# A scheduler's duration table in a cross-attention and MoE-LoRA kernel, with transposes modelled as holding the SP queue

## The chip, the core and the metric

The kernel runs on one core of a Trainium2 chip. The metric is the device time of one execution in microseconds (us). One execution was also recorded by the hardware profiler; the profile's lines come from it. Engine names in the profile are PE (TensorE matmul), PEld (its weight load), DVE (VectorE), ACT (ScalarE), POOL (GpSimd) and SP (SyncE, which here only issues DMAs).

## What is computed

There are two batches of 1024 rows; rows are 2048 wide. `fake_quant` rounds to 0..255 and scales back.

```
x = x + fake_quant(layernorm(x)) @ fake_quant(ctx)        # GEMM 1, 2048 x 2048 per batch
y = layernorm(x)
w = top-2 softmax weights of y @ W_router.T               # 8 experts, rank 16
x = x + y @ W_base.T + b_base + 2 * sum_e w_e (y @ A_e.T) @ B_e.T    # GEMM 2 with LoRA
```

## The kernel before

**Tasks and a planner.** The kernel does not issue instructions as it goes through its loops. Each helper adds a task to a `Plan` (L88): an engine, an assumed duration, the tiles that it reads and writes, and for a DMA an assumed transfer time. `rank` gives each task a due time, counted back from the due times of its matmuls. `order` (L141) then plays the tasks through in modelled time: whenever an engine is modelled as free, it takes the ready task with the earliest due time whose tile slots are free. The tasks are emitted in the order of their modelled starts (L1133), so each engine's program order is what the model found best. The hardware keeps that order on each engine; an engine that waits for one tile holds up everything behind it. An elementwise scaling (`affine`, L339) may run on ACT or on DVE; DVE takes it only where the model has ACT busy. 3048 tasks are ordered.

The model of a DMA has three numbers: how long SP is busy issuing (0.47 us for a load, 1.25 for a transpose), how long the transfer takes on one shared DMA resource (`dma_free`: the bytes at 360e3 a us; a transpose 0.896 us per 1024 columns), and when its tile counts as landed (2.0 after). At most 8 transfers are outstanding, and none is issued when the resource is booked more than 2.5 us ahead.

**All loads, stores and transposes go through SP's one queue, in one order.** That is the order around which the change works.

**GEMM 1.** For each batch x is loaded in row tiles of 128, its mean and variance are taken on DVE (`stats`), the inverse root by Newton steps on POOL, ACT quantises it to u8 (`q8`), `qn` is the f16 copy without the zero point, and an SP transpose makes `at`, the stationary operand. The context is loaded (`bs`), quantised on DVE (`u`, L357), made f16 on ACT or DVE (`b`, L346 or L355). `gemm1` (L630) issues 128x128x512 matmuls into one of 8 PSUM banks (`g`) and DVE adds the result to x (L657).

**GEMM 2** is a Strassen-like product. For each pair p of row tiles, `y_prep` (L725) normalises four blocks of x (`yt_a`) and forms the sums s1 to s4. Each of a11, a12, a22, s1, s2, s3 and s4 is split into a high and a low f16 half (`nat_a`, `nat_s`: the copy is L346 on ACT, the subtraction L742 on DVE) and transposed by SP (L336) into `y_a` or `y_s`. `comb` is L749. x tiles are stored to DRAM (`spill`) and loaded again later (`xr`).

The weights come in rows. For each of two column halves cp, four groups grp (0 to 3) and eight steps k, `w_step` (L889) loads `wt` and `wb` (or `ws`), combines them on DVE (L918; L928 and L932; L939 and L942 by group), scales the high half (L346 on ACT or L353 on DVE) and computes the low half on DVE (L902). `g2` (L1021) runs the three matmuls per product (L1032) for the four row pairs, and after the last step adds the LoRA product (L1046) and lets DVE add the banks X and Y to x (L1057). Names like "grp 1 tile k" below mean the weight tile of that group and step.

**Router.** `hmm` (L780) multiplies y_a and y_s with the LoRA and router matrix (`ph`, L790 and L794, 16 narrow matmuls each), ACT copies and DVE adds the halves into `hf` (L806, L809). After the last of them the softmax and the top-2 weights run, and one SP transpose makes `hT`. `load_lb` prepares the LoRA output weights (`lb`), `add_bias` adds the bias to the x tiles (L978).

The first row tile is preceded by 30 warm-up matmuls (L609).

Of the kernel before, what the change touches and what calls it, by code (L numbers as in the profile page):

```python
# [21 lines left out]
P = 128  # L22
# [6 lines left out]
KT = D // P  # L29
# [14 lines left out]
MM = 0.216  # L44
# [7 lines left out]
EV1 = 5.0  # L52
SP_D = 10.0
HC = 4.0
PUT = 10.0
# [10 lines left out]
HOP = 0.7  # L66
DMA_SLACK = 3.0


# [13 lines left out]
class Task:  # L83
    __slots__ = ("eng", "dur", "durs", "fn", "preds", "succs", "prio", "cap", "bufs", "left",
                 "ready", "start", "done", "dma", "seq", "pe", "far", "need")


class Plan:  # L88
    def __init__(self):
        self.tasks = []  # L90

    def add(self, eng, dur, fn, r=(), w=(), prio=None, cap=None, dma=None, far=None):
# [7 lines left out]
        t.far = far  # L100
# [24 lines left out]
        self.tasks.append(t)  # L125
        return t
# [14 lines left out]
    def order(self):  # L141
# [51 lines left out]
        while todo:  # L193
# [8 lines left out]
            for eng in busy:  # L202
                while busy[eng] <= now:
# [66 lines left out]
def xattn_ffn_kernel(ctx, tc, x, cx, scal, wT, bias, arT, bT, out):  # L270
# [60 lines left out]
    def load(dst, dst_ap, src, nbytes, w, r=(), **kw):  # L331
        add("SP", 0.47, lambda: nc.sync.dma_start(dst_ap(), src() if callable(src) else src),
            r=r, w=w, dma=nbytes * P / 360e3, **kw)

    def transpose(dst, src, r, w, cols, **kw):
        add("SP", 1.25, lambda: nc.sync.dma_start_transpose(dst(), src()),  # L336
            r=r, w=w, dma=0.896 * cols / 1024, **kw)

    def affine(dst, src, n, r, w, scale=None, bias=None, only=None, **kw):  # L339
        ptrs = sum(v is not None and not isinstance(v, float) for v in (scale, bias))  # L340

        def fn(eng):
            get = lambda v: v() if callable(v) else v
            o, i, a, c = dst(), src(), get(scale), get(bias)
            if eng == "ACT":
                nc.scalar.activation(  # L346
                    o, i, AF.Copy if c is None else AF.Identity,
                    scale=1.0 if a is None else a, bias=0.0 if c is None else c,
                )
# [12 lines left out]
        return add(durs, 0, fn, r=r, w=w, **kw)  # L362
# [46 lines left out]
    def prep_lora(when):  # L409
# [59 lines left out]
        for q in range(2):  # L469
            s1, s2 = a32[q], a32[q + 2]  # L470
            split(s1, q)
            split(s2, q + 2)
            add("DVE", 0.6,
                lambda s1=s1, s2=s2: nc.vector.tensor_tensor(
                    s1.ap(), s2.ap(), s1.ap(), ALU.subtract), r=[s2], w=[s1])
            split(s1, q + 4)

    def prep_bmax():
        m = buf("sm", [P, 52], F32, "sm_bmax")
        for h in range(2):  # L480
            s = buf("u", [P, HD], F32, f"bms_{h}")
            load(s, s.ap, bT[:, h * HD : (h + 1) * HD], HD * 4, [s])
            add("DVE", 1.13,
                lambda s=s, h=h: nc.vector.tensor_reduce(
                    m.ap()[:, h : h + 1], s.ap(), AX.X, ALU.max, apply_absolute_value=True),
                r=[s], w=[m])
# [26 lines left out]
    def w_norm(cp, when):  # L513
        acc = buf("wacc", [P, 24], F32, f"wacc_{cp}", KT)
        for n, k in enumerate(range(KT - 1, -1, -1)):
# [6 lines left out]
            def sq(eng, s=s, d=d, k=k):  # L522
# [7 lines left out]

            add({"ACT": 1.2, "DVE": 1.3}, 0, sq, r=[s], w=[d, (acc, [k])],
                prio=when + WN_STEP * n)
# [33 lines left out]
    def ln1(S, b, i):  # L566
# [3 lines left out]
        for h in range(2):  # L570
            add("DVE", 1.2, lambda h=h: stats(xt[h], s, 0, h), r=[xt[h]], w=[s])
        add("DVE", 0.8, lambda: rstd_seed(s, 1), w=[s])
# [57 lines left out]
    def gemm1(S, b, i, c, t):  # L630
# [29 lines left out]

        add("DVE", 0.78, evac, r=[ps], w=[(xb, [c % 2]), (s, [j])], cap=t + KT * MM + EV1)
        if c % 2 == 0:
# [19 lines left out]
        sq = buf("q8", [P, HD], U8, f"sq_{b}_{i}_{c}")  # L682
        add("ACT", 1.3, lambda: square(c // 2), r=[xb], w=[(s, [j]), sq])

# [40 lines left out]
    def y_prep(S, b, p):  # L725
# [10 lines left out]
        def emit(o, t):  # L736
# [3 lines left out]
            affine(lambda: n.ap()[:, 0], t.ap, HD, [t], [n])  # L740
            add("DVE", 1.13,
                lambda: nc.vector.tensor_tensor(  # L742
# [5 lines left out]
        def comb(dst, a, c, op):  # L748
            add("DVE", 1.13, lambda: nc.vector.tensor_tensor(dst.ap(), a.ap(), c.ap(), op),  # L749
                r=[a, c], w=[dst])  # L750
# [138 lines left out]
    def w_step(S, b, cp, grp, k):  # L889
# [10 lines left out]
        def lo(src, lo, up, r):  # L900
            add("DVE", 0.14 + 0.00104 * (up - lo),
                lambda: nc.vector.scalar_tensor_tensor(  # L902
                    w.ap()[:, 1, lo:up], src(), g, w.ap()[:, 0, lo:up], ALU.mult,
                    ALU.subtract),
                r=r + [sc_r], w=[w])
# [10 lines left out]
        if grp == 0:  # L916
            add("DVE", 0.6,
                lambda: nc.vector.tensor_tensor(  # L918
# [3 lines left out]
        elif grp == 1:  # L922
# [3 lines left out]
                 C * 4, [(bot, [1])])  # L926
            add("DVE", 0.6,
                lambda: nc.vector.tensor_tensor(  # L928
                    bot.ap()[:, :C], top.ap()[:, :C], top.ap()[:, C:], ALU.subtract),
                r=[top], w=[(bot, [0])])  # L930
            add("DVE", 0.6,
                lambda: nc.vector.tensor_tensor(  # L932
# [3 lines left out]
        else:  # L936
            bot = load_wrow(HK + k, cp, f"wb_{n}", far=WFAR)
            add("DVE", 1.13,
                lambda: nc.vector.tensor_tensor(bot.ap(), bot.ap(), top.ap(), ALU.subtract),  # L939
                r=[top], w=[bot])  # L940
            add("DVE", 0.6,
                lambda: nc.vector.tensor_tensor(  # L942
# [4 lines left out]
    def load_lb(S, b, cp, js):  # L947
        s = buf("u", [P, HD], F32, f"lbs_{b}_{cp}_{js[0]}")
        load(s, s.ap, bT[:, cp * HD : (cp + 1) * HD], HD * 4, [s])
        for j in js:  # L950
# [5 lines left out]
            if j == 2:  # L956
                add("DVE", 0.6,
                    lambda: nc.vector.tensor_tensor(
                        s.ap()[:, :C], s.ap()[:, :C], s.ap()[:, C:], ALU.subtract), w=[s])
            g = sB[:, cp : cp + 1]  # L960
            add("ACT", 0.62,
                lambda lb=lb, src=src: nc.scalar.activation(
                    lb.ap()[:, 0], src(), AF.Copy, scale=g), r=[s, (scale_b, [cp])], w=[lb])
            add("DVE", 0.67,
                lambda lb=lb, src=src: nc.vector.scalar_tensor_tensor(
# [4 lines left out]
    def add_bias(S, b, cp, t):  # L970
# [4 lines left out]
        for i in [2 * p + 1 for p in range(NP)] + [2 * p for p in range(NP)]:  # L975
            xb = S["c", cp, i]
            add("DVE", 1.13,
                lambda xb=xb: nc.vector.tensor_tensor(xb.ap(), xb.ap(), bb.ap(), ALU.add),  # L978
# [12 lines left out]
    def put(S, b, cp, i, t):  # L991
        xb = S["c", cp, i]
        last = b == NB - 1 and cp == 1 and i % 2 == 0
        for c in range(2):
# [4 lines left out]
            else:  # L999
                cs, parts = slice(0, HD), [0, 1]  # L1000
            add("SP", 0.47,
                lambda cs=cs: nc.sync.dma_start(
                    out[b, i * P : (i + 1) * P, cp * HD + cs.start : cp * HD + cs.stop],
                    xb.ap()[:, cs]),
                r=[(xb, parts)], dma=4 * (cs.stop - cs.start) * P / 360e3, prio=t + PUT)

# [14 lines left out]
    def g2(S, b, cp, grp, k, p, t):  # L1021
# [30 lines left out]
        for bk, tt, c in EVAC[grp] + ((("Y", 0, 1),) if split and not grp else ()):  # L1052
# [7 lines left out]

            add("DVE", 0.72, ev, r=[ps, (scale_b, [cp])], w=[(xb, [c])], cap=t + EV2)
        if grp == 2:
# [125 lines left out]
```

## Time and profile before

| | us |
|---|---|
| three runs | 967.72, 965.92, 967.12 |
| their median | 967.12 |
| span of the profiled execution | 965.8 |
| PE busy in it | 913.9 |
| DVE, ACT, POOL busy | 734.1, 379.9, 100.0 |
| DMA, mean rate | 252 GB/s |

A line "L1032 PE ..." is a group of instructions of line 1032 of the kernel. An idle time in brackets with "<-" is the time for which the engine had nothing to do before the instruction, and what ended it. A line of a waits view reads: engine and line, what it waited for, us in total, times, longest. "SPq" is SP's queue: the instruction's duration there is the time for which it held the queue. A clock of 0.50 in a row means that a matmul takes twice as long.

### The profile page before, as it was taken

What the parts mean: (1) busy time and instruction counts of PE and PEld (TensorE: products, weight loads), DVE (VectorE), ACT (ScalarE), POOL (GpSimd) and SP (SyncE); (2) the same over time, 40 slices, a digit from 0 to 9 for tenths busy, and PEclk for the clock granted to TensorE, in tenths of its full rate; (3) what the DMA queues carried; (4) which work ended last, traced back from release to release, by engine and by line L of the source; (5) the groups of instructions that cost most, each with busy time, mean ns of one, the idle gap of its engine ahead of it and who ended that gap; (6) DMA issues with size and microseconds to landing.
All of it is one profiled execution on the core that took longest, in us unless ns stands there. A gap on an engine that the chain in (4) does not pass through costs nothing.

```text
span 965.8 us, 12426 instructions
## 1 busy us (share of the span) xinstructions
PE 913.9 (95%) x4478; PEld 431.5 (45%) x4478; DVE 734.1 (76%) x1229; ACT 379.9 (39%) x440; POOL 100.0 (10%) x353
## 2 busy tenths in 40 slices
PE   3699998997999999999999999997898999999998
PEld 1245445454444444444444444545543444444443
DVE  7579887996988876999555778987597876699231
ACT  3466785641425422243555644641230321225000
POOL 3405431000000000005220223000000000000000
PEclk9799999999999999999999999999999999999999
DMA  9999999899899986966999979899978479695011
GB/s 319 246 392 336 303 313 243 214 189 233 246 302 389 360 312 244 363 219 242 239 273 356 319 190 228 245 215 185 255 180 262 163 272 325 207 356 171 34 66 66
DMA packets 225518, 243.12 MB, mean 252 GB/s; under 512 B 160944, under 2 KB 162992, under 8 KB 225456
## 3 DMA queue, kind: packets, MB, share of 16 engines
q1 hardware_dynamic: 225456, 242.33, 83.0%
q8 instruction: 35, 0.57, 0.2%
q14 instruction: 27, 0.22, 0.1%
HBM read 172.03 MB, written 31.46 MB: 211 GB/s over the span
## 4 chain that ended last, share of the span: by engine, by line
PE 62%; DVE 19%; POOL 6%; DMA 5%; issue 5%; ACT 2%; SPq 1%; DVEq 0%; POOLq 0%; ACTq 0%
PE X L1032 28%; PE Y L1032 19%; PE g L636 11%; DVE yt_a L749 2%; DVE nat_s L742 2%; DVE w L902 2%; PE X L1046 2%; PE Y L1046 2%; DVE nat_a L742 2%; DMA wb<-in_wT_dram 2%; DVE xr L1057 1%; POOL sm L399 1%; POOL sm L395 1%; DMA wt<-in_wT_dram 1%; DVE x L657 1%
## 5 line engine op out<-in xcount | busy, mean ns | idle before, releaser
L636 PE MATMUL g<-b,at 128*128 128x512 f16 x1024 | 228.5, 386 | 9.2 <-ACT b L346 7.4
L1032 PEld LDWEIGHTS <-y_s 128*128 128x128 f16 x1536 | 149.8, 98 | 192.4 <-issue 9.9
L1032 PE MATMUL Y<-w,y_s 128*128 128x512 f16 x768 | 207.1, 380 | 5.7 <-DVE hf L809 2.8
L1032 PE MATMUL X<-w,y_s 128*128 128x512 f16 x768 | 207.7, 381 | 4.3 <-DVE w L902 2.6
L1032 PE MATMUL X<-w,y_a 128*128 128x512 f16 x768 | 190.4, 380 | 4.5 <-DVE w L902 2.6
L1032 PEld LDWEIGHTS <-y_a 128*128 128x128 f16 x1152 | 112.5, 98 | 144.9 <-issue 7.3
L636 PEld LDWEIGHTS <-at 128*128 128x128 f16 x1024 | 101.4, 99 | 133.6 <-issue 17.5
L346 ACT ACTIVATE w<-wb,gW 128x1024 f16<-128x1024 f32 x59 | 67.4, 1147 | 190.3 <-DVE wb L932 94.3
L1032 PE MATMUL Y<-w,y_a 128*128 128x512 f16 x384 | 103.3, 379 | 3.8 <-DVE xr L1057 2.7
L902 DVE SCALAR_TENSOR_TENSOR w<-wb,gW,w 128x1024 f16<-128x1024 f32 x64 | 81.6, 1278 | 11.7 <-ACT w L346 11.3
L357 DVE TENSOR_SCALAR u<-bs,rec,sc 128x1024 uint8<-128x1024 f32 x64 | 50.9, 808 | 27.5 <-DMA bs<-in_cx_dram 22.0
L346 ACT ACTIVATE b<-u,nz 128x1024 f16<-128x1024 uint8 x47 | 53.0, 1143 | 44.7 <-DVE u L357 40.2
L1057 DVE SCALAR_TENSOR_TENSOR xr<-X,uW,xr 128x512 f32<-128x512 f32 x70 | 50.5, 744 | 25.7 <-PE X L1046 23.2
L1057 DVE SCALAR_TENSOR_TENSOR xr<-Y,uW,xr 128x512 f32<-128x512 f32 x45 | 33.2, 742 | 36.0 <-PE Y L1046 36.0
L657 DVE SCALAR_TENSOR_TENSOR x<-g,s,x 128x512 f32<-128x512 f32 x64 | 47.4, 745 | 10.3 <-PE g L636 10.1
L346 ACT ACTIVATE q<-x,sm 128x1024 uint8<-128x1024 f32 x32 | 38.0, 1232 | 34.0 <-POOL sm L584 29.2
L928 DVE TENSOR_TENSOR wb<-wt 128x512 f32<-128x512 f32 x32 | 21.9, 687 | 34.4 <-DMA wt<-in_wT_dram 28.7
L939 DVE TENSOR_TENSOR wb<-wb,wt 128x1024 f32<-128x1024 f32 x32 | 38.7, 1218 | 11.5 <-DMA wb<-in_wT_dram 11.5
L742 DVE TENSOR_TENSOR nat_s<-yt_a,nat_s 128x1024 f16<-128x1024 f32 x32 | 38.3, 1217 | 5.5 <-ACT nat_s L346 5.5
L367 DVE BATCH_NORM_STATS2 sm<-x 128x6 f32<-128x512 f32 x64 | 40.4, 680 | 2.5 <-DMA x<-in_x_dram 2.4
L346 ACT ACTIVATE nat_s<-yt_a 128x1024 f16<-128x1024 f32 x27 | 27.8, 1049 | 33.3 <-DMA y_s<-nat_s 14.9
L790 PE MATMUL ph<-ar,y_a 128*128 128x272 f16 x192 | 37.0, 284 | 3.9 <-DVE xr L1057 2.1
(157 smaller groups left out, 901.8 us busy)
## 6 DMA issues: line engine op xcount, KB each, us to landing
wt<-in_wT_dram SPq DMA_DIRECT2D x88, 512.0 KB, 6.4
bs<-in_cx_dram SPq DMA_DIRECT2D x64, 512.0 KB, 9.9
wn<-in_wT_dram SPq DMA_DIRECT2D x32, 512.0 KB, 7.6
wb<-in_wT_dram SPq DMA_DIRECT2D x32, 512.0 KB, 8.1
x<-in_x_dram SPq DMA_DIRECT2D x30, 512.0 KB, 8.3
spill<-x SPq DMA_DIRECT2D x28, 512.0 KB, 4.0
xr<-spill SPq DMA_DIRECT2D x28, 512.0 KB, 6.8
out_dram<-xr SPq DMA_DIRECT2D x24, 512.0 KB, 4.2
```

The source lines that it names most:

```text
L346: nc.scalar.activation(o, i, AF.Copy if c is None else AF.Identity, scale=1.0 if a is None else a, bias=0.0 if c is None else c,)
L357: nc.vector.tensor_scalar(o, i, a, c, ALU.mult, ALU.add)
L367: nc.vector.bn_stats(st[:, 2 * h + c], b.ap()[:, c * C : (c + 1) * C])
L636: nc.tensor.matmul(ps.ap(), aT.ap()[:, k, :], S["b", c, k // 4].ap()[:, k % 4, :], start=k == 0, stop=k == KT - 1,)
L657: nc.vector.scalar_tensor_tensor(xs, ps.ap(), s12, xs, ALU.mult, ALU.add, accum_out=s.ap()[:, o : o + 1])
L742: lambda: nc.vector.tensor_tensor(n.ap()[:, 1], t.ap(), n.ap()[:, 0], ALU.subtract), r=[t], w=[n])
L790: nc.tensor.matmul(ph.ap()[:, : 2 * AR], y[half].ap()[:, 0, k, :], ar[:, kr, :], start=kk == 0, stop=False,)
L902: lambda: nc.vector.scalar_tensor_tensor(w.ap()[:, 1, lo:up], src(), g, w.ap()[:, 0, lo:up], ALU.mult, ALU.subtract),
L939: lambda: nc.vector.tensor_tensor(bot.ap(), bot.ap(), top.ap(), ALU.subtract),
L1032: nc.tensor.matmul(ps.ap(), y.ap()[:, a, k, :], w.ap()[:, q, j * C : (j + 1) * C], start=k == 0 and fresh and i == 0, stop=k == HK - 1 and ...
L1046: nc.tensor.matmul(ps.ap(), hT.ap()[:, 2 * p + tt, a], lb.ap()[:, q], start=False, stop=i == 2, skip_group_check=True,)
L1057: nc.vector.scalar_tensor_tensor(xs, ps.ap(), uW[:, cp : cp + 1], xs, ALU.mult, ALU.add)
```

## The change

Only numbers and rules of the planner change. No task is added or removed, none does other work; the program's order and the choice between ACT and DVE follow from the new model. The line numbers of the kernel after are larger by 3 to 7.

- A transpose is modelled as holding SP until the modelled transfers ahead of it are through and its own time (0.35 + 0.6 us per 1024 columns) has passed; its tile lands 2.4 us later. Before, it held SP 1.25 us whatever was ahead.
- Another DMA holds SP 0.4 us for 0.47, starts 0.2 us after issue (1.1 after its start before), moves 405e3 bytes a us for 360e3, and lands 1.8 us later for 2.0.
- Most DVE durations and three ACT durations in the table grow by 0.03 to 0.18 us. PE's and POOL's are left.

```
+RATE = 405e3
+LAND = 1.8
+TURN_LAND = 2.4
...
                     end = now + t.dur
-                    busy[eng] = end
-                    wake(end)
                     if t.dma is not None:
-                        dma_free = max(now + 1.1, dma_free) + t.dma
-                        t.done = dma_free + 2.0
+                        if t.turn:
+                            dma_free = end = max(now + 0.3, dma_free) + t.dma
+                            t.done = dma_free + TURN_LAND
+                        else:
+                            dma_free = max(end + 0.2, dma_free) + t.dma
+                            t.done = dma_free + LAND
                         lanes = [x for x in lanes if x > now] + [t.done]
                     else:
                         t.done = end + 0.2
+                    busy[eng] = end
+                    wake(end)
                     wake(t.done)
...
     def load(dst, dst_ap, src, nbytes, w, r=(), **kw):
-        add("SP", 0.47, lambda: nc.sync.dma_start(dst_ap(), src() if callable(src) else src),
-            r=r, w=w, dma=nbytes * P / 360e3, **kw)
+        add("SP", 0.4, lambda: nc.sync.dma_start(dst_ap(), src() if callable(src) else src),
+            r=r, w=w, dma=nbytes * P / RATE, **kw)
 
     def transpose(dst, src, r, w, cols, **kw):
         add("SP", 1.25, lambda: nc.sync.dma_start_transpose(dst(), src()),
-            r=r, w=w, dma=0.896 * cols / 1024, **kw)
+            r=r, w=w, dma=0.35 + 0.6 * cols / 1024, turn=True, **kw)
...
-        durs = {"ACT": n * 0.00083 + 0.19 + 0.09 * ptrs, "DVE": n * 0.00053 + 0.08 + 0.06 * ptrs}
+        durs = {"ACT": n * 0.00083 + 0.19 + 0.09 * ptrs, "DVE": n * 0.00053 + 0.145 + 0.06 * ptrs}
```

The other durations that change, each in its own line: a DVE subtraction or addition of 1024 columns (L742, L749, L939, L978) and the reduction in the preparation 1.13 to 1.22; one of 512 columns (L918, L928, L932, L942, L958) 0.6 to 0.69; `stats` 1.2 to 1.38; GEMM 1's eviction L657 0.78 to 0.84; GEMM 2's eviction L1057 0.72 to 0.75; L902 0.14 to 0.215 plus 0.00104 a column; the squares 1.3 to 1.33 (ACT, L675) and 1.2 and 1.3 to 1.25 and 1.31 (ACT and DVE); `lb` 0.62 to 0.72 (ACT) and 0.67 to 0.75 (DVE).

More of the change, by code (lines that the diff above doesn't have):

```diff
@@ L84 @@
     __slots__ = ("eng", "dur", "durs", "fn", "preds", "succs", "prio", "cap", "bufs", "left",
-                 "ready", "start", "done", "dma", "seq", "pe", "far", "need")
+                 "ready", "start", "done", "dma", "seq", "pe", "far", "need", "turn")
 class Plan:
@@ L90, in __init__, with add @@
         self.tasks = []
-    def add(self, eng, dur, fn, r=(), w=(), prio=None, cap=None, dma=None, far=None):
+    def add(self, eng, dur, fn, r=(), w=(), prio=None, cap=None, dma=None, far=None, turn=False):
         t = Task()
@@ L99, in add @@
         t.pe = prio if eng == "PE" else None
-        t.far = far
+        t.far, t.turn = far, turn
         def spans(accs):
@@ L472, in prep_lora @@
             split(s2, q + 2)
-            add("DVE", 0.6,
+            add("DVE", 0.69,
                 lambda s1=s1, s2=s2: nc.vector.tensor_tensor(
@@ L482, in prep_bmax @@
             load(s, s.ap, bT[:, h * HD : (h + 1) * HD], HD * 4, [s])
-            add("DVE", 1.13,
+            add("DVE", 1.22,
                 lambda s=s, h=h: nc.vector.tensor_reduce(
@@ L529, in sq @@
                     )
-            add({"ACT": 1.2, "DVE": 1.3}, 0, sq, r=[s], w=[d, (acc, [k])],
+            add({"ACT": 1.25, "DVE": 1.31}, 0, sq, r=[s], w=[d, (acc, [k])],
                 prio=when + WN_STEP * n)
@@ L570, in ln1 @@
         for h in range(2):
-            add("DVE", 1.2, lambda h=h: stats(xt[h], s, 0, h), r=[xt[h]], w=[s])
+            add("DVE", 1.38, lambda h=h: stats(xt[h], s, 0, h), r=[xt[h]], w=[s])
         add("DVE", 0.8, lambda: rstd_seed(s, 1), w=[s])
@@ L659, in evac @@
             )
-        add("DVE", 0.78, evac, r=[ps], w=[(xb, [c % 2]), (s, [j])], cap=t + KT * MM + EV1)
+        add("DVE", 0.84, evac, r=[ps], w=[(xb, [c % 2]), (s, [j])], cap=t + KT * MM + EV1)
         if c % 2 == 0:
@@ L682, in gemm1 @@
         sq = buf("q8", [P, HD], U8, f"sq_{b}_{i}_{c}")
-        add("ACT", 1.3, lambda: square(c // 2), r=[xb], w=[(s, [j]), sq])
+        add("ACT", 1.33, lambda: square(c // 2), r=[xb], w=[(s, [j]), sq])
     def ln2(S, b, p):
@@ L740, in emit @@
             affine(lambda: n.ap()[:, 0], t.ap, HD, [t], [n])
-            add("DVE", 1.13,
+            add("DVE", 1.22,
                 lambda: nc.vector.tensor_tensor(
@@ L748, in comb @@
         def comb(dst, a, c, op):
-            add("DVE", 1.13, lambda: nc.vector.tensor_tensor(dst.ap(), a.ap(), c.ap(), op),
+            add("DVE", 1.22, lambda: nc.vector.tensor_tensor(dst.ap(), a.ap(), c.ap(), op),
                 r=[a, c], w=[dst])
@@ L900, in lo @@
         def lo(src, lo, up, r):
-            add("DVE", 0.14 + 0.00104 * (up - lo),
+            add("DVE", 0.215 + 0.00104 * (up - lo),
                 lambda: nc.vector.scalar_tensor_tensor(
@@ L916, in w_step @@
         if grp == 0:
-            add("DVE", 0.6,
+            add("DVE", 0.69,
                 lambda: nc.vector.tensor_tensor(
@@ L926, in w_step @@
                  C * 4, [(bot, [1])])
-            add("DVE", 0.6,
+            add("DVE", 0.69,
                 lambda: nc.vector.tensor_tensor(
@@ L930, in w_step @@
                 r=[top], w=[(bot, [0])])
-            add("DVE", 0.6,
+            add("DVE", 0.69,
                 lambda: nc.vector.tensor_tensor(
@@ L937, in w_step @@
             bot = load_wrow(HK + k, cp, f"wb_{n}", far=WFAR)
-            add("DVE", 1.13,
+            add("DVE", 1.22,
                 lambda: nc.vector.tensor_tensor(bot.ap(), bot.ap(), top.ap(), ALU.subtract),
                 r=[top], w=[bot])
-            add("DVE", 0.6,
+            add("DVE", 0.69,
                 lambda: nc.vector.tensor_tensor(
@@ L956, in load_lb @@
             if j == 2:
-                add("DVE", 0.6,
+                add("DVE", 0.69,
                     lambda: nc.vector.tensor_tensor(
@@ L960, in load_lb @@
             g = sB[:, cp : cp + 1]
-            add("ACT", 0.62,
+            add("ACT", 0.72,
                 lambda lb=lb, src=src: nc.scalar.activation(
                     lb.ap()[:, 0], src(), AF.Copy, scale=g), r=[s, (scale_b, [cp])], w=[lb])
-            add("DVE", 0.67,
+            add("DVE", 0.75,
                 lambda lb=lb, src=src: nc.vector.scalar_tensor_tensor(
@@ L976, in add_bias @@
             xb = S["c", cp, i]
-            add("DVE", 1.13,
+            add("DVE", 1.22,
                 lambda xb=xb: nc.vector.tensor_tensor(xb.ap(), xb.ap(), bb.ap(), ALU.add),
@@ L1000, in put @@
                 cs, parts = slice(0, HD), [0, 1]
-            add("SP", 0.47,
+            add("SP", 0.4,
                 lambda cs=cs: nc.sync.dma_start(
@@ L1004, in put @@
                     xb.ap()[:, cs]),
-                r=[(xb, parts)], dma=4 * (cs.stop - cs.start) * P / 360e3, prio=t + PUT)
+                r=[(xb, parts)], dma=4 * (cs.stop - cs.start) * P / RATE, prio=t + PUT)
     GROUPS = (
@@ L1059, in ev @@
                 )
-            add("DVE", 0.72, ev, r=[ps, (scale_b, [cp])], w=[(xb, [c])], cap=t + EV2)
+            add("DVE", 0.75, ev, r=[ps, (scale_b, [cp])], w=[(xb, [c])], cap=t + EV2)
         if grp == 2:
```

## The prediction

> **What bounds the kernel now.** I read the page's busy times first, then busy time by stage, then waits, chain and timelines of the stages where TensorE (PE) is not full.
>
> ```profile
> span 965.8 us, 12426 instructions
> ...
> PE 913.9 (95%) x4478; PEld 431.5 (45%) x4478; DVE 734.1 (76%) x1229; ACT 379.9 (39%) x440; POOL 100.0 (10%) x353
> ```
>
> PE is without work for 965.8 - 913.9 = 52 us. A change of order can only move these, or time in which PE ran at half clock. Busy time by stage (columns: stretch, its length, PE, PEld, DVE, ACT, POOL, clock, DMA share, GB/s) says where they are:
>
> ```profile
> 0.00:47.00 47.00, 23.25 (x68) 8.60 (x69) 31.33 (x71) 19.31 (x17) 18.03 (x62) 0.85 0.95 280
> ...
> 160.00:205.00 45.00, 39.95 (x211) 19.26 (x209) 43.13 (x75) 23.67 (x26) 0.40 (x1) 1.00 0.94 224
> 205.00:245.00 40.00, 34.52 (x225) 19.66 (x224) 32.10 (x44) 10.40 (x14) 0.00 (x0) 0.96 0.96 227
> ...
> 620.00:694.00 74.00, 64.03 (x400) 35.92 (x399) 55.09 (x84) 23.59 (x28) 0.00 (x0) 0.98 1.00 238
> 694.00:745.00 51.00, 48.26 (x223) 21.59 (x222) 42.20 (x81) 12.15 (x13) 0.00 (x0) 1.00 0.77 221
> ```
>
> PE misses 23.8 us in startup, 5.1 + 5.5 in batch 0's change of GEMM, 10.0 + 2.7 in batch 1's; from 325 to 620 it is busy throughout. Next, what the SP queue does in these stages: the transposes' line (min/median/max of one, ns), and SP's timeline.
>
> ```profile
> L336 SPq DMA_TRANSPOSE y_s<-nat_s x32: 1359/2500/8552, 137.7 to 722.7; - x32
> ```
>
> ```profile
> 217.44 14.10 SPq L336 DMA_TRANSPOSE y_s<-nat_s  x5
> 231.60 0.83 SPq L332 DMA_DIRECT2D wt<-in_wT_dram  x1
> ```
>
> Five transposes hold the queue 14.1 us (2.8 each; the planner believed 1.25), and the weight load behind them leaves at 231.60. DVE, whose next instruction needs it, stands. The same follows in batch 1, here in the chain (start, length, what):
>
> ```profile
> 680.51 5.71 DMA wt<-in_wT_dram
> 686.25 0.70 DVE wb L928
> ...
> 726.15 6.46 DMA wb<-in_wT_dram
> ...
> 733.85 1.40 DVE xr L1057 x2
> ```
>
> PE's timeline has the price, in brackets on the right:
>
> ```profile
> 690.47 0.81 PE L1032 MATMUL Y<-w,y_s 128*128 128x512 f16 x3 [2.79 <-DVE hf L809]
> ```
>
> ```profile
> 734.65 0.82 PE L1032 MATMUL Y<-w,y_a 128*128 128x512 f16 x3 [1.89 <-DVE xr L1057]
> ```
>
> PE did not wait for that weight tile: it waited for short DVE work (the router's add L809, the evictions L1057) that the planner had put behind the DVE instruction that waited for the load:
>
> ```profile
> 732.70 1.22 DVE L939 TENSOR_TENSOR wb<-wb,wt 128x1024 f32<-128x1024 f32 x1 [6.29 <-DMA wb<-in_wT_dram]
> 733.85 0.74 DVE L1057 SCALAR_TENSOR_TENSOR xr<-Y,uW,xr 128x512 f32<-128x512 f32 x1
> ```
>
> **The change part by part.** No instruction's work changes and none is added or taken out: 3048 tasks before and after. So every duration edit has no cost of its own, and acts through the order and the choice of ACT or DVE alone. Set side by side task by task, PE keeps 1103 of 1269 places (no move over 14 places), SP 389 of 503 (none over 4), POOL all. DVE and ACT change most: 42 tasks go from DVE to ACT, 28 the other way. I take each stage where PE waits, follow the new order through the old durations, and count the change in PE's time.
>
> *Startup, 0 to 47.* Three more cx loads go ahead of the first transpose (landing near 24.5 for 20.4), and half a dequantised b tile goes behind a q pass on ACT, so the first real matmuls start near 38 instead of 31.05. But the last b tile no longer stands behind both normalised rows, so PE then runs on, without the 3.43 us it waited until 41.27. By 46.9 I count 36 to 37 matmuls both ways: **0**, bounds -2 and +3.
>
> *85 to 112.* Two of the at transposes go behind stores and wn loads; at number 4 is issued near 91.1 for 85.9. Its first use had 4.9 us of slack, its successors 2.4 to 3.2: 0 if all slack holds, +3 if one misses by its slack again. I take **0**, nearest to the slack rows; the next stage swallows a little lateness anyway.
>
> *160 to 245.* The first weight tile of GEMM 2 is late already: PE's waits for L902 are 5.2 us in three.
>
> ```profile
> PE X L1032 <- DVE w L902: 5.2, 3, 2.6
> ```
>
> In the new order the subtraction L918 and a copy stand with L902 on DVE, 1.4 us more, for a DVE that is 43.13 of 45 us busy. Behind it the transposes still precede the same wt load, and L902 of the third grp 1 tile goes behind L928 and L932 of later tiles (0.69 + 0.69 a pair): ready near 243.4 for 241.8. That wait is behind all the earlier ones, so it alone counts: **+1.6**, bounds -2 (the y_s waits of 205 to 245 shrink) and +5 (it adds to the 1.4 and the slack lost before).
>
> *245 to 325.* One gap of 0.43 us goes (a wb load passes a transpose). Three hi copies move to ACT, but DVE takes L939 of tiles 6 and 7 (1.22 each) ahead of L902 of tile 5, which comes to 305.0 where PE wanted it at 302.9: +2.1 - 0.43, **+1.6**, bounds -1 and +3. From 325 to 620 the nearest slack I found is 8.6 us: 0.
>
> *628 to 694.* The evictions L1057 of group 0 go ahead of two nat_s subtractions (1.22 each): the gap of 2.06 us at 658 falls to some 0.6, **-1.5**. The router's adds L809 and the last three evictions go ahead of the L928 that waits for the wt load: PE's gaps of 1.85, 0.98, 2.79 and 0.52 (6.1) go. What is late next is the y_s2 tile of rows 2 and 3, whose transpose is itself in the queue; I charge one hold, the row's median 2.5: **-3.6**. Bounds for both together -7.6 (nothing late next) and -1 (each gap has a new owner).
>
> *725 to 740.* The wt and wb loads of tile 2 pass the last y_s3 transpose, and the evictions stand ahead of L939: gaps of 1.89, 0.33 and 0.52 go, **-2.7**, bounds -2.7 and 0. The tail, 3.8 us of eviction and store after the last matmul, stays.
>
> Sum: 0 + 0 + 1.6 + 1.6 - 1.5 - 3.6 - 2.7 = -4.6 on the profiled execution: 965.8 to 961.2. The runs' median is 967.12, 1.3 above that span, so **962.5**.
>
> The clock is left at 0 in this sum. It fell to half right after the gap at 658:
>
> ```profile
> 661.30:664.70 3.40, 3.40 (x18) 2.13 (x17) 3.03 (x4) 0.00 (x0) 0.00 (x0) 0.50 0.04 7
> ```
>
> 3.4 us at 0.50 cost 1.7. If the gap caused it, its going saves 1.7; a new gap elsewhere may cost as much: bounds -1.7 and +1.7, and 0 stands midway. [...]
>
> [...]
>
> **The rivals.**
>
> *Batch 1's gain comes whole.* Nothing is late after the removed stalls (-1.5 - 6.1 - 2.7 = -10.3) and batch 0 costs 1 to 3: 965.8 - 8.3 + 1.3 = 958.8; with batch 0 neutral and the clock's 1.7 saved, 955. For it: the holds are the same in both batches, and PE's gaps there are all DVE order. Against: between 620 and 694 the DMA share is 1.00, so the next transpose is never far.
>
> *No change.* The wt load still stands behind the transposes (SP moves nothing over 4 places), DVE still idles 7 us for it, and each removed PE wait is taken over by the next late tile: batch 1 gives -3, batch 0 takes +3: 967.
>
> *Slower: DVE's weight work becomes the bound of batch 0.* Where the new order puts L939 and L942 of later tiles (1.22 + 0.69) ahead of L902 of the tile that PE wants, each such step without slack costs PE 1.9 us. 160 to 325 has some 24 steps and DVE is 146 of 165 us busy. Four such steps are +7.6; with half of batch 1's gain (-3.9), 967.12 + 3.7 = 970.8. It decides from three late steps on, if batch 1 gives no more than half. For it: two such steps are in my sum already. Against: between 245 and 325 PE lost only 1.1 us so far.
>
> *The model doesn't hold.* It makes every transpose wait for the modelled transfers ahead, but one of 1024 columns at 14.53 was through in 1.3 us with loads outstanding; then the order is shuffled without aim: between the last two cases.
>
> **How the numbers follow.** This kernel's measurement tells about 0.2% (1.9 us) from no change, so same is 965.2 to 969.0. The forecast, batch 0 a few us late and batch 1 most of its gaps rid, 960 to 965: 0.43. The whole gain, below 960: 0.17. No change: 0.13. Slower, 969 to 974: 0.27. The range 955.5 to 970.5 takes the whole gain down to its end, and the slower case up to four late steps; the forecast's own range is 958.5 to 965.
>
> **What would show it.** Right: no PE waits for L809 at 665 to 693, and none for xr L1057 behind L939 at 730; DVE idles for wt and wb loads as before, 28.7 and 11.5 us, without PE behind it; PE's waits for L902 grow from 5.2 us to some 8. Wrong: PE waits for y_s grow in batch 1 by more than 2.5 us; the start of real matmuls after 40 us; at transposes that PE waits for near 96; or more than three waits for L902 between 245 and 325.

## The result and the profile after

The kernel after takes 972.54 us (median of 4 runs, 970.43 to 972.85), before 967.42 in the runs beside it: a ratio of 1.0051, interval 1.0037 to 1.0066. It is slower by half a per cent; the forecast was faster by as much. The page's first lines of after:

```profile
span 970.5 us, 12450 instructions
...
PE 913.2 (94%) x4478; PEld 430.3 (44%) x4478; DVE 728.5 (75%) x1217; ACT 395.2 (41%) x452; POOL 91.1 (9%) x353
```

PE does the same 913 us of work and stands 57 us for 52. Busy time by stage of after (stretch, length, PE, PEld, DVE, ACT, POOL, clock, DMA share, GB/s):

```profile
47.00:160.00 113.00, 108.82 (x537) 52.77 (x536) 86.30 (x207) 80.08 (x107) 28.66 (x113) 0.98 1.04 305
160.00:205.00 45.00, 38.35 (x226) 19.91 (x224) 40.04 (x70) 28.72 (x32) 0.40 (x1) 1.00 0.87 211
205.00:245.00 40.00, 34.24 (x231) 19.74 (x230) 30.73 (x38) 9.13 (x12) 0.00 (x0) 1.00 0.98 206
245.00:325.00 80.00, 73.27 (x323) 32.26 (x323) 67.54 (x108) 35.43 (x46) 0.00 (x0) 0.96 0.93 296
...
620.00:694.00 74.00, 72.10 (x486) 42.36 (x484) 62.12 (x94) 32.68 (x39) 0.00 (x0) 1.00 0.97 219
```

Batch 1's change of GEMM is cured (72.10 of 74 for 64.03). But 47 to 160, where PE never stood before, has lost 4.2, and 245 to 325 now 6.7 for 1.1. Which waits are new, PE's waits of after say (total, times, longest):

```profile
PE g L643 <- DMA at<-qn: 6.3, 2, 4.2
PE g L643 <- ACT b L353: 5.3, 2, 3.1
PE X L1039 <- DVE w L909: 5.3, 3, 2.5
PE Y L1039 <- DMA y_s<-nat_s: 3.0, 4, 1.5
PE Y L1039 <- DVE hf L816: 2.9, 1, 2.9
PE Y L1039 <- DVE w L909: 2.7, 3, 1.2
```

A wait alone does not say what it cost in the end. So I set the times beside each other at which PE, in the trace of each kernel, starts its n-th task (the PE tasks are the same 1269 in all). The table has the lateness against before (us; plus is later) at eight such points, named by their times in before, for after and for every experiment; all are profiled executions. One execution stands behind each row: second_half has before's order up to the middle and is still up to 2.0 us off 0 there, and rate_only's profiled execution took 977.25 us where the median of its runs is 980.73. So a difference of 2 us or less between two rows is not shown by them.

| | 76.0 | 128.0 | 185.2 | 251.4 | 330.5 | 620.1 | 706.7 | 956.0 |
|---|---|---|---|---|---|---|---|---|
| after | -2.8 | +3.2 | +4.8 | +9.5 | +12.2 | +12.3 | +6.2 | +4.8 |
| second_half | -0.1 | -0.1 | -1.2 | -2.0 | -0.8 | -0.8 | -7.1 | -9.1 |
| start_and_second | -2.4 | -2.4 | -3.1 | -3.7 | -2.9 | -2.9 | -10.7 | -10.8 |
| table_only | -2.5 | -2.5 | +0.1 | +1.4 | +3.2 | +3.2 | -3.6 | -5.5 |
| model_only | -0.1 | +4.1 | +1.8 | +0.4 | +7.6 | +12.1 | +14.0 | +14.4 |
| hold_only | -1.0 | -0.6 | +1.5 | +0.8 | +1.5 | +1.5 | +6.4 | +3.1 |
| rate_only | -2.2 | +3.0 | +2.9 | +7.5 | +6.6 | +9.1 | +10.9 | +9.7 |
| table_hold | -1.4 | -1.4 | -1.0 | -0.6 | +2.5 | +2.5 | -5.0 | -6.1 |
| th_rate | -1.5 | -0.5 | +1.8 | +5.6 | +7.0 | +7.0 | -2.0 | -1.9 |
| th_land | -1.0 | -1.1 | -0.6 | +2.5 | +5.3 | +5.3 | -2.1 | -3.4 |
| rate_395 | -1.4 | +0.8 | +2.9 | +7.5 | +10.6 | +10.6 | +3.5 | +1.4 |
| rate_320 | -2.3 | +2.3 | +5.6 | +6.5 | +8.2 | +8.2 | +0.3 | +1.7 |
| w_first | -2.0 | +2.8 | +3.9 | +4.5 | +9.8 | +9.9 | +4.5 | +2.4 |
| at_first | -2.0 | -1.6 | +6.9 | +11.2 | +14.8 | +14.8 | +9.8 | +6.6 |
| at_first_both | -2.8 | -1.5 | +3.5 | +7.2 | +10.4 | +10.4 | +1.5 | +1.3 |
| both_repairs | -2.8 | -2.0 | +3.2 | +3.9 | +9.7 | +9.7 | +2.0 | +2.1 |
| three_repairs | -1.6 | -1.1 | +3.0 | +4.8 | +9.8 | +9.8 | +4.3 | +3.0 |

So after gains 2.8 us in startup, loses 15 between there and 330 us, keeps that through PE's full stretch, and gets 7.5 back in batch 1.

### The profile page after: what moved, and what is told of

Same layout as the page of the kernel before. It is cut to its first block, busy times and chain, and to the rows that moved or that the text cites. A ratio compares the mean times of both kernels' runs of the same rounds, so it can differ in the third digit from the quotient of the medians.

```text
span 970.5 us, 12450 instructions
## 1 busy us (share of the span) xinstructions
PE 913.2 (94%) x4478; PEld 430.3 (44%) x4478; DVE 728.5 (75%) x1217; ACT 395.2 (41%) x452; POOL 91.1 (9%) x353
## 4 chain that ended last, share of the span: by engine, by line
PE 52%; DMA 14%; DVE 13%; issue 4%; POOL 3%; ACT 3%; SPq 2%; DVEq 0%; POOLq 0%; ACTq 0%
PE X L1039 25%; PE Y L1039 18%; PE g L643 5%; DMA bs<-in_cx_dram 4%; DMA y_s<-nat_s 3%; DVE w L909 2%; DMA wt<-in_wT_dram 2%; DMA wn<-in_wT_dram 2%; PE X L1053 2%; SPq L343 2%; PE Y L1053 2%; DVE yt_a L756 1%; DVE nat_s L749 1%; DVE x L664 1%; DMA out_dram<-xr 1%
## 5 line engine op out<-in xcount | busy, mean ns | idle before, releaser
L643 PEld LDWEIGHTS <-at 128*128 128x128 f16 x1024 | 100.6, 99 | 135.0 <-issue 10.7
L353 ACT ACTIVATE w<-wb,gW 128x1024 f16<-128x1024 f32 x64 | 72.9, 1146 | 196.0 <-DVE wb L949 85.5
L909 DVE SCALAR_TENSOR_TENSOR w<-wb,gW,w 128x1024 f16<-128x1024 f32 x64 | 81.5, 1280 | 21.1 <-ACT w L353 20.9
L353 ACT ACTIVATE b<-u,nz 128x1024 f16<-128x1024 uint8 x49 | 55.3, 1143 | 42.1 <-DVE u L364 37.7
L756 DVE TENSOR_TENSOR yt_a<-yt_a,yt_a 128x1024 f32<-128x1024 f32 x32 | 38.2, 1218 | 5.6 <-ACT yt_a L353 5.6
L353 ACT ACTIVATE nat_s<-yt_a 128x1024 f16<-128x1024 f32 x30 | 30.7, 1048 | 25.8 <-DMA y_a<-nat_a 9.4
L935 DVE TENSOR_TENSOR wb<-wt 128x512 f32<-128x512 f32 x32 | 22.0, 687 | 25.2 <-DMA wt<-in_wT_dram 24.9
```

Of the source, the lines that this page charges most:

```text
L353: nc.scalar.activation(o, i, AF.Copy if c is None else AF.Identity, scale=1.0 if a is None else a, bias=0.0 if c is None else c,)
L643: nc.tensor.matmul(ps.ap(), aT.ap()[:, k, :], S["b", c, k // 4].ap()[:, k % 4, :], start=k == 0, stop=k == KT - 1,)
L756: add("DVE", 1.22, lambda: nc.vector.tensor_tensor(dst.ap(), a.ap(), c.ap(), op), r=[a, c], w=[dst])
L909: lambda: nc.vector.scalar_tensor_tensor(w.ap()[:, 1, lo:up], src(), g, w.ap()[:, 0, lo:up], ALU.mult, ALU.subtract),
```

## The experiments

### Does each half stand by itself?

The program order is only a list, so it can be cut. In the middle, at one matmul of batch 0 where PE is busy throughout, the lists of before and after have the same tasks behind them (one differs). Two kernels emit a written list: `second_half` has before's order up to there and after's from there; `start_and_second` has, besides, after's order up to the first matmul of the second context tile.

```
-        for task in plan.order():
-            task.fn(task.eng) if len(task.durs) > 1 else task.fn()
+        for seq, eng in ORDER:
+            plan.tasks[seq].fn(eng) if len(plan.tasks[seq].durs) > 1 else plan.tasks[seq].fn()
```

> The order of before up to the middle of the work (PE is busy throughout there in both traces), the order of after from there on. Theory A (each half's order acts by itself: after's order costs 12.2 us up to 320 us and gives 7.5 us back in batch 1): 967.4 - 7.5 = 960, no PE wait for L809 near 690 above 1 us more than in after. Rival B (batch 1 only gives back lateness, since a late PE finds its tiles ready; an on-time PE would meet the old waits): 967 within 2 us, with PE's waits near 670 to 735 back.

> After's order up to the first matmul of the second context tile (near 44 us), before's order until the middle, after's from there. Theory A: after's startup is 2.85 us faster at 47 us, and this is kept until the first weight tile of GEMM 2, so 960 - 2.9 = 957. Rival: the first weight tile is bound by POOL and the weight norms (before: PE waits 2.6 us for it at 167.8), not by PE, so an earlier PE only waits longer there: 959 to 960, with PE's wait for L902 near 165 up from 2.6 to some 5 us.

Measured: 958.61 us, 0.9926 of before (0.9911 to 0.9941), and 957.24, 0.9913 (0.9898 to 0.9929). Theory A holds for the halves: batch 1's gain is its own, not lateness given back. Both are faster than before and after. The three orders also place the loss: after and second_half differ in their order up to the middle alone, and in their ratios by 1.25% (12 us); start_and_second has after's startup too and loses nothing by it, so the loss lies between the startup and the middle. Of the 2.9 us expected of the startup the traces have 2.1 (-2.9 at 330 us against -0.8), and the two timed intervals overlap. PE's wait for the first weight tile did not grow:

```profile
164.28 0.59 PE L1032 MATMUL X<-w,y_a 128*128 128x512 f16 x2 [2.62 <-DVE w L902]
```

This is start_and_second, 3.5 us earlier than before's 167.79 with the same wait: the chain to that tile moves with PE's GEMM 1, whose results it needs.

### Which part of the edit does what?

`table_only` has the new durations and the old DMA model, `model_only` the reverse. `hold_only` has of the DMA model only `turn` and the transposes' numbers, `rate_only` only the rest (the diff is rate_only's against model_only):

```
     def transpose(dst, src, r, w, cols, **kw):
-            r=r, w=w, dma=0.35 + 0.6 * cols / 1024, turn=True, **kw)
+            r=r, w=w, dma=0.896 * cols / 1024, **kw)
```

> Only the durations of DVE and ACT are new; transposes and other DMAs are modelled as before. The order that comes out has the router's adds and the evictions ahead of the DVE instruction that waits for the weight load in batch 1, as after has. Theory (the longer DVE durations brought batch 1's gain, not the transposes' hold): batch 1 gains 6 to 8 us; up to 320 us it loses some, since two at transposes stand behind wn loads here too: 962 to 970 in all. Rival (the transposes' hold brought the gain): PE's gaps near 670 to 735 stay as in before, 967 to 975.

> Only the DMA model is new (transposes hold SP, rate, landing); durations are the old ones. Here the router's adds still stand behind the DVE instruction that waits for the weight load. Theory (the table brought the gain): batch 1 keeps its PE gaps of some 10 us or more; the at transposes behind wn loads cost 2 to 6 near 102 us: 969 to 976. Rival (the hold brought the gain): batch 1 gains 6 to 8 us as in after: 962 to 968.

Measured: table_only 964.02, 0.9979 (0.9965 to 0.9993); model_only 982.56, 1.0178 (1.0160 to 1.0195), slower than I had expected. From 620 us to the end table_only gains 8.7 us and model_only loses 2.3. In the table every kernel with the new durations gains there, 6.5 to 9.2 us, and every one with the old durations loses, 0.6 to 2.3. The durations brought batch 1's gain, not the hold. PE's timeline shows it at the router's add, first in table_only, then in hold_only:

```profile
688.46 1.44 PE L1032 MATMUL Y<-w,y_s 128*128 128x512 f16 x3 [3.17 <-DVE hf L809]
```

```profile
690.18 0.39 PE L797 MATMUL ph<-ar,y_s 128*128 128x272 f16 x1 [7.97 <-DVE hf L816]
```

With the longer durations the planner puts all of these adds but at most the last, and the three evictions, ahead of the DVE instruction that waits for the weight load; with the old ones two or three adds and the evictions stay behind it. The one that is left in table_only, on DVE:

```profile
687.51 0.69 DVE L928 TENSOR_TENSOR wb<-wt 128x512 f32<-128x512 f32 x1 [6.70 <-DMA wt<-in_wT_dram]
688.12 0.29 DVE L809 TENSOR_TENSOR hf<-ph,hf 128x136 f32<-128x136 f32 x1
```

It costs PE the 3.17 us above; after has the same place, with 2.91.

> Old durations; of the DMA model only the transposes' hold is new (and their 0.35 + 0.6 and 2.4 us); load rate 360, start, landing and issue as before. In the order that comes out all four late at transposes are ahead of the first wn load, as in before. Theory (it is the faster rate and landing, 405 against a mean of 252 measured, that lets loads pass ahead of transposes and costs the 15 us of the DMA model): no PE wait for at near 102, 965 to 972. Rival (the hold itself costs them): 975 to 985.

> Old durations; of the DMA model all but the transposes' hold is new (rate 405, issue 0.4, start and landing). Two of the four late at transposes stand behind the first wn load. Theory (rate and landing cost the 15 us): a PE wait of 2 us or more for at near 102, and 972 to 982. Rival (the hold costs them): 965 to 969.

Measured: hold_only 972.42, 1.0060 (1.0039 to 1.0081); rate_only 980.73, 1.0149 (1.0124 to 1.0173). Neither extreme is right: with the old durations the hold costs 0.6% and the rest 1.5%, the latter as rate_only's theory had it. The profile has 3.1 us of the hold's 5.7, about half by 330 us (+1.5) and half in batch 1, where the wait of 7.97 above stands; amounts so small the table cannot place.

With the new durations under them it is otherwise. `table_hold` is after with the old rate, issue, start and landing; `th_rate` has the new rate as well, `th_land` the new issue, start and landing:

```
-RATE = 405e3
-LAND = 1.8
+RATE = 360e3
+LAND = 2.0
...
-                            dma_free = max(end + 0.2, dma_free) + t.dma
+                            dma_free = max(now + 1.1, dma_free) + t.dma
...
-        add("SP", 0.4, lambda: nc.sync.dma_start(dst_ap(), src() if callable(src) else src),
+        add("SP", 0.47, lambda: nc.sync.dma_start(dst_ap(), src() if callable(src) else src),
```

> After without the new rate, start, landing and issue times of DMAs: new durations and the transposes' hold remain. All late at transposes and the LN2 statistics are ahead of the first wn work. Theory (the new rate and landing are what costs; the table brings batch 1's gain): no PE wait for at near 102, batch 1 as in after, 957 to 966. Rival (the hold costs by itself as it did with the old durations, +5.7): 967 to 973.

> New durations, the transposes' hold and the new rate of 405e3; issue, start and landing as before. The last at transposes and the square of the first wn tile stand as early as in after. Theory (the rate lets wn loads and their squares go early): lateness of 5 to 9 us by 333 us, batch 1 gains 8: 966 to 971. Rival (start and landing do it): as without the new rate, 960 to 964.

> New durations, the transposes' hold and the new issue, start and landing times; rate 360e3. All late at transposes and the LN2 statistics are ahead of the first wn work. Theory (the rate is what costs): 959 to 965, no wait for at near 102. Rival (start and landing cost): 966 to 971, with lateness of 5 us or more by 252 us.

Measured: table_hold 962.13, 0.9964 (0.9946 to 0.9981); th_rate 967.71, 1.0007 (0.9996 to 1.0019); th_land 963.82, 0.9961 (0.9946 to 0.9976). Beside table_only's 0.9979 the hold is worth nothing that the intervals tell. The rate alone costs some 0.4%, start and landing alone nothing, and both together (after) 0.9%: more than their sum.

### Is it the rate, or luck of the order?

Two kernels are after with one number changed.

> After with the modelled rate at 395e3 for 405e3, a change of 2.5%. Theory (systematic: loads modelled too fast go too early): the same order features as after at 102 us and the same time, 970 to 975. Rival (any change of a number reshuffles the order, and the time moves by luck of 1%): a time off after's 972.5 by more than 4 us either way.

> After with the modelled rate at 320e3, nearer to the measured mean of 252 GB/s. All late at transposes are ahead of the first wn load. Theory (a slower modelled rate takes the loss away): 958 to 966. Rival (luck of the order): anything from 960 to 980, with the lost time at new places.

Measured: rate_395 968.72, 1.0031 (1.0014 to 1.0048); rate_320 969.33, 1.0032 (1.0017 to 1.0046). Neither expectation for 395 came: the time is under 970, and less than 4 us from after's. Its interval overlaps after's, so the 0.2% between them are not shown. The theory fails at 320: the wait for at near 102 is gone as expected, but 8 us are lost in batch 0 all the same (+5.6 at 185), in PE's waits for b and before the matmuls `arn` at 90 to 98 (3.7 us) and for y_a at 161 to 168 (5.0). th_land belongs beside these two, since it is after with the rate at 360: the ratios are 1.0032 at 320, 0.9961 at 360, 1.0031 at 395 and 1.0051 at 405. The time does not follow the modelled rate in one direction: it falls by 0.7% and rises by 0.7% between neighbours. So luck of the order may be worth that much, and no run tells it from an effect of the rate. A slower modelled rate is no cure by itself, so "modelled too fast" is at most a part.

### Three places, repaired by hand

The three are in after's own trace. First, SP ahead of PE's longest new wait (start, time held, what), the wait, and the clock behind it in two stretches:

```profile
95.70 2.02 SPq L339 DMA_DIRECT2D wn<-in_wT_dram  x2
97.88 8.28 SPq L343 DMA_TRANSPOSE at<-qn  x2
```

```profile
106.21 5.96 PE L643 MATMUL g<-b,at 128*128 128x512 f16 x19 [4.18 <-DMA at<-qn]
```

```profile
106.21:109.90 3.69, 3.69 (x12) 1.50 (x13) 2.86 (x12) 3.59 (x8) 0.00 (x0) 0.67 1.07 289
109.90:114.00 4.10, 4.10 (x19) 1.73 (x17) 1.49 (x7) 1.18 (x3) 2.69 (x11) 0.88 1.01 256
```

The first of the two transposes holds SP from 97.88 to 104.14, just before the second wn load ahead of it lands (104.37). The wait of 4.2 and the clocks of 0.67 and 0.88 (3.69 x 0.33 + 4.10 x 0.12 = 1.7) make the 6.0 us of the table between 76 and 128. DVE stands there too, for a square of the same wn tile that the planner put ahead of LN2's statistics:

```profile
104.39 1.22 DVE L534 SCALAR_TENSOR_TENSOR wn<-wn 128x1024 f32<-128x1024 f32 x1 [7.00 <-DMA wn<-in_wT_dram]
```

Second, DVE at the third grp 1 tile of batch 0, and PE behind it:

```profile
241.96 0.69 DVE L935 TENSOR_TENSOR wb<-wt 128x512 f32<-128x512 f32 x1 [6.71 <-DMA wt<-in_wT_dram]
242.57 1.22 DVE L756 TENSOR_TENSOR yt_a<-yt_a,yt_a 128x1024 f32<-128x1024 f32 x1
...
246.02 0.69 DVE L935 TENSOR_TENSOR wb<-wt 128x512 f32<-128x512 f32 x1 [1.03 <-DMA wt<-in_wT_dram]
246.63 0.68 DVE L939 TENSOR_TENSOR wb<-wb 128x512 f32<-128x512 f32 x1
247.23 1.28 DVE L909 SCALAR_TENSOR_TENSOR w<-wb,gW,w 128x1024 f16<-128x1024 f32 x1
```

```profile
248.56:252.60 4.04, 4.04 (x10) 1.47 (x10) 3.97 (x7) 1.15 (x1) 0.00 (x0) 0.50 0.97 377
```

L909 comes to 248.51, and twelve matmuls from there run at half clock: they start 0.427 us apart, where those of 701.92 to 704.51, at full clock, start 0.216 apart (12 x 0.211 = 2.5 us). Third, in before the first nat_s subtraction stood ahead of the evictions near 205, in after behind all seven.

The lists were edited so: in `at_first` SP's wn loads 15 and 14 go behind the last at transpose; in `at_first_both` their squares on ACT and DVE go back too; in `w_first` the sum L756 goes ahead of the waiting L935, and the L935 of tile 4 behind L909 of tile 2; `both_repairs` joins the last two; `three_repairs` puts the first two nat_s subtractions ahead of the evictions besides.

> After's order with one move: the first two wn loads (tiles 15 and 14) go behind the last two at transposes on SP. Theory (PE's wait of 4.18 us at 102 and the 1.85 us of half clock behind it come from at number 6, held 6.26 us behind these two loads): no wait above 0.5 us at 102 and full clock after it; of the 6 us some come back at the first weight tile of GEMM 2, so 967 to 970. Rival (the spill stores ahead hold it as long): the wait stays above 2 us and the time within 1 us of after, 971.5 to 973.5.

> The earlier move of the two wn loads behind the at transposes, and this time the squares that read them go back too: on ACT behind the last arT copy before 109 us, on DVE behind the first LN2 statistics (L703). Theory (moving the loads alone made DVE stand 12 us for wn at 110 and LN2's statistics and POOL's Newton steps late, so the first weight tile came at 174.8 for 172.8): DVE's wait for wn at 110 falls below 2 us, the first weight tile comes by 169, and the time is 965 to 969. Rival (something later than the Newton steps binds the first weight tile): the tile stays at 172 or later, 971 to 976.

> After's order with two moves on DVE: in the third grp 1 step the yt_a sum L756 goes ahead of the wait for the weight load, and L935 of grp 1 tile 4 behind L909 of tile 2. Theory (PE's waits of 1.62 and 2.52 us at 244 to 248 come from these two instructions of 1.2 and 0.7 us and the wait of 1.0 for tile 4's load): L909 of tile 2 ends near 246 for 248.5, and PE's half clock from 246 to 253 goes or shrinks: 967 to 970. Rival (the late weight load alone sets it): PE starts on tile 2 within 0.5 us of after, 972 to 973.

> After's order with both repairs: the two wn loads and their squares behind the late at transposes and the LN2 statistics, and the two DVE moves at 240. Theory (these two places carry most of after's loss in batch 0): the repairs add, 2.5 and 1.5 us off after's 972.5, to 966 to 969, near before or just above. Rival (the second repair is taken back once PE arrives earlier): as with the first alone, 969 to 972.

> After's order with both earlier repairs and a third: on DVE the first two nat_s subtractions (L749, 1.2 each) go ahead of the first L935 of grp 1 and the seven evictions L1064 (0.74 each), where before had the first of them. Theory (the evictions ahead of them made the y_s transposes, and with them the wt load of the third grp 1 tile, 4 to 5 us late): the first y_s2 transpose leaves by 208 for 212.8, the wt load lands by 238 for 240.5, and the time falls from 968.7 to 964 to 967. Rival (the evictions are now late and PE waits for its banks, or the later transposes wait for their own sources): the wt load lands no earlier than 240, or a new wait of 1.5 us or more stands at 208 to 222, and the time stays at 967.5 to 970.

Measured against before: at_first 976.12, 1.0101 (1.0077 to 1.0125); at_first_both 969.97, 1.0049 (1.0033 to 1.0064); w_first 971.01, 1.0041 (1.0026 to 1.0055); both_repairs 968.67, 1.0015 (1.0002 to 1.0029); three_repairs 970.46, 1.0025 (1.0010 to 1.0041).

at_first took the wait at 102 away but for 0.26 us and became slower than after. The loads went later and DVE still stood for them, ahead of the statistics of LN2:

```profile
110.29 1.22 DVE L534 SCALAR_TENSOR_TENSOR wn<-wn 128x1024 f32<-128x1024 f32 x1 [12.09 <-DMA wn<-in_wT_dram]
```

LN2's Newton steps on POOL (115.40 for 110.39) and the weight norms' sum behind them (168.12 for 166.03) came later, and PE, 1.6 us early at 128, was 6.9 late at 185. With the squares moved too the DVE wait is 2.61 and PE 3.5 late for after's 4.8, a difference that the table does not tell from noise, and the ratio 1.0049 is no different from after's 1.0051 by its interval. My theory of 965 to 969 failed. The traces have a lead that no run followed up: the moves brought LN2's statistics forward for the first pair of row tiles alone. Those of the second pair start on DVE at 120.8 in before, 131.2 in after and 130.5 in at_first_both, behind subtractions for y_a and y_s and GEMM 1's evictions. In all the runs where they start by 124.4 PE is at most 1.8 late at 185; where they start at 129.4 or later it is 1.8 to 6.9 late; the two at 125.5 are 0.1 and 5.6 late. That the one makes the other is not shown. The second repair alone does what was expected of its place (4.5 for 9.5 late at 251), but the 5 us are lost again by 330 (9.8 late), where L909 of later tiles is late (PE waits 2.4 at 293, and half clock follows: two matmuls from 293.29 take 0.84 us, two from 246.39 took 0.59). Together the repairs take the ratio from 1.0051 to 1.0015, though the trace has only 2.5 of the 15 us of batch 0 back (9.7 late at 330). The third brought nothing: the rival was right on the load, and the time is just above its range (970.46 for 967.5 to 970). The first y_s2 transpose left at 211.68 and not by 208, since SP took a wt load at 211.24 ahead of it, and the wt load landed at 240.33 for 240.45. The eight y_s transposes behind it fill SP until then anyway:

```profile
218.94 0.83 SPq L339 DMA_DIRECT2D wb<-in_wT_dram  x1
219.87 17.01 SPq L343 DMA_TRANSPOSE y_s<-nat_s  x6
236.99 0.51 SPq L339 DMA_DIRECT2D wt<-in_wT_dram  x1
```

These lines are of after: six transposes in 17.0 us, 2.8 each, as before.

## Why the prediction was wrong

*Batch 1 was right in mechanism and, partly by luck, in its sum.* Forecast -1.5 - 3.6 - 2.7 = -7.8, measured -7.5 (from +12.3 at 620 to +4.8). The parts were off both ways: up to 706.7 us -6.1 for -5.1, behind it -1.4 for -2.7. The owners differ: the last add L816 (L809 of before) still stands behind the waiting instruction and costs 2.9 us, against my sign of being right, where I had charged 2.5 for a y_s2 tile; the wait at 738 is 0.95, and the half clock near 661 is gone but five slow matmuls come at 699. The cause that I gave, evictions and adds ahead of the waiting DVE instruction, is shown but for that add; that it comes from the durations, not from the transposes' hold, I had not said.

*The step that failed first is "85 to 112 ... I take 0, nearest to the slack rows", with bounds 0 and +3.* It measured +6.0: 4.2 of wait and 1.7 of half clock. My sign of being wrong, PE waiting for at transposes near there, came. I had followed at number 4, and it was in time; number 6 stood behind two wn loads that had moved ahead of it, and I priced its hold by slack instead of by the landing of the loads in front. The row for it was at hand: a transpose of before held 8.55 us (the maximum in the line that I showed) behind six such loads. I also looked at SP's order alone. The squares that read these loads had moved ahead of LN2 on ACT and DVE, and at_first, slower without the wait than after with it, shows that this is as costly.

*The second is "160 to 245 ... ready near 243.4 ... it alone counts: +1.6".* The tile came at 248.51, and from 128 to 251 PE lost 6.3. I let the wt load land when it landed before (237.17); it landed at 241.94, since the whole chain to it was late, and the half clock of twelve matmuls came on top. "It alone counts" holds up by the numbers: +1.6 and the 4.8 by which the wt load landed later are 6.4 of the 6.7 us by which the tile came later (248.51 for 241.8). What I left out was to move the chain by PE's lateness.

*245 to 325*: +1.6, measured +2.7, in bounds. *Startup*: 0, measured -2.8; I counted 36 to 37 matmuls by 46.9 both ways; PE started on its full run at 36.34 and did some 13 more by 47 than in before. It ran five slow matmuls there instead of the 24 in before's two stretches, which my count, with the clock at 0, did not have.

The sum of these misses, -2.8 + 6.0 + 4.7 + 1.1 + 0.3 = +9.3, is the distance from -4.6 to +4.7.

*The rivals.* The slower one named DVE's weight work and 970.8. Its sign, PE's waits for the low half of w, came true in part: 5.9 to 8.0 us for X and Y together, but the 5.2 that the prediction names are X alone, and X went to 5.3. The place came true too; but the wait for at and the half clock, which it lacked, were as much again, and batch 1 gave 7.5 us where it had 3.9. That 970.8 is near the 972.54 measured is luck. The clock term, kept at 0 with bounds of 1.7, was too narrow: past the startup after has three stretches at half clock, which cost some 1.7, 2.5 and 1.1 us, and before two of 1.7 each (at 231 and 661), so it was about +1.9.

*Settled and open.* Shown: batch 1's gain belongs to the durations, after's loss to its order between the startup and the middle, and of the DMA numbers the rate of 405 costs alone, with start and landing more. Not settled: which instructions of batch 0 make the rest, and whether it is the numbers or luck of the order. The first two repairs of single places gave back 2.5 of 15 us, the third nothing, and the next late tile took over; and the rate's effect goes up and down.

## What to carry to other kernels

A planner's numbers act through the order alone, and each stage answers by itself: price a change by stage, cut the two orders where the bound engine is full, and keep the better half of each (here 957 us, from halves of 967 and 972). Where an in-order queue gets a load earlier, follow the load's readers on every engine as well as the transfers behind it: the reader stands ahead of other work and waits with the engine (in after DVE stood 7.00 us for a wn tile, and the transpose behind two wn loads held SP for 6.26). A more faithful cost in a greedy planner is no reason to expect a better order; the same hold was worth nothing with one duration table and cost 0.6% with another.

## What the runs showed of the hardware

A transpose's hold went with the transfers in front of it: in after 6.26 us behind two wn loads that landed 7.4 and 7.8 after their issue, and 2.8 us each in a row of six. Past the startup, 132 of the 133 transposes of before and after that were issued with transfers open gave SP back between 0.6 us before and 1.8 after the last of these landed, the other 3.0 after. In the startup some were free earlier: the one at 14.53 in before, after 1.34 us, 3.7 before the last load in front of it landed. So in these two traces the hold past the startup tells of the transfers in front.

Between startup and end the granted clock fell to half in or just behind PE waits of 1.39 to 4.18 us. In after it fell at 107.43, behind the one of 4.18 that ended at 106.21; at 247.38, in the second of two of 1.62 and 2.52 with one matmul between, and twelve slow matmuls follow at 249; and at 697.94, in the one of 2.91 from 695.8, and five follow at 699. In before it fell behind one of 1.39, with slow matmuls from 231.2 to 234.6, and at 661.29, behind one of 2.06 that ended at 660.08; but not after the 2.62 at 165 or the 2.79 at 687.7. With the same order there, second_half fell to half after 2.39 at 166 and not after 1.37 at 229. Length alone does not decide it in these traces. Between startup and end, every stretch at half clock in the traces of before and after is 3.41 or 6.83 us long (before: 231.21 to 234.62, 661.29 to 664.70; after: 107.43 to 110.85, 247.38 to 254.21, 697.94 to 701.35).
